# A graph layer that gathers rows by POOL and fetches single rows by SP and ACT: 74 single rows a step instead of 24

## The chip, the core and the metric

One core of a Trainium2 chip runs the whole program. The metric is the time of one execution on the device in microseconds (us), of which the median over several runs is given. One execution is taken with the hardware profiler, and the lines shown come from it. Engines: PE multiplies matrices, DVE and ACT work on vectors, POOL issues the indirect gathers, SP and ACT issue plain transfers; each engine works through its own instructions in their order, and the engines wait for one another by semaphores.

## The reference

There are 50,000 nodes with 128 numbers each and 1,650,000 edges, sorted by their destination; the last of each node's edges is that of the node to itself. Every edge has one of two types, which chooses the weights of its message.

```python
def _L0_gnn_ref(X, edge_index, edge_types, W_data, b_data, W_control, b_control, W_self, b_self):
    src, dst = (edge_index[0], edge_index[1])
    Xs = X[src]
    m_data = Xs @ W_data.T + b_data
    m_ctrl = Xs @ W_control.T + b_control
    msg = jnp.where((edge_types == 0)[:, None], m_data, m_ctrl)
    agg = jax.ops.segment_sum(msg, dst, num_segments=X.shape[0])
    out = agg + (X @ W_self.T + b_self)
    return jax.nn.relu(out)
x = _layernorm(x + _L0_gnn_ref(x, edge_index, edge_type_2, ...), axis=-1)
```

## The kernel before

The edges are cut into blocks, a block into two steps (`Q = 2`). A step sums the rows of its edges' sources by destination and type, and for this it needs these rows of `x` in SBUF. Its edges come by three ways:

- 12 x 128 edges are **gathered**: POOL issues one indirect transfer for 128 rows (L478), 24 of them in a block. A pass is 6 gathers into one tile `y`, of which there are 10, and PE multiplies each 128 rows with a matrix of zeros and ones (`oh`) that says where a row belongs (L497).
- `F = 43` edges are **fillers**. An edge of a node to itself needs no gather, since that row lies in the block's window of `x_t`; DVE puts a filler in its place in the lists (`fill`, L310 to L340).
- `S` edges are **single rows**: SP and ACT fetch each with a transfer of its own, 512 bytes (L452). `TURNS` says how many rows of a step each of the two takes, here 12 and 12.

The single rows' numbers are loaded for ten blocks at a time (`one_g`, L166). DVE makes byte addresses of those of one block (`offsets`, tile `at_x`, L436), a list of `X = Q * S` whole numbers on one partition, at partition `AT`: first SP's for both steps, then ACT's. In `single_rows` each queue loads its addresses from this list into registers (L447, one instruction for a stretch of the list) and then, for each row, sets a register and issues the copy. `LOADS` cuts this work into parts. With `LOADS = 1` each queue does it in one stretch, for a block that is `AHEAD = 2` blocks later. PE waits for both queues' rows of a block at the end of its first step (`rows_fetched`, L461) and multiplies them with one more part of `oh` (L503).

Blocks 0 and the last are plain: they have neither fillers nor single rows. The number of blocks follows from how many edges one holds:

```python
CE = Q * SIZE                      # SIZE = 12 * 128
BE = CE + Q * F + X
NBLK = 2 + (E - CE) // BE
```

The order of every engine's work is written out by hand in the loop over the blocks (L615). In block b, four passes run. After the first, PE does the layer of block b - 1 (`layer`, L528), DVE its moments and the matrix `oh` of block b + 2. After the second come ACT's root of block b - 1 (`root`, L552) and DVE's `counts`. After the third come DVE's `store` of block b - 1 (L558, which reads the root) and its `fill` of block b + 5. After the fourth, DVE makes the addresses for block b + 3 (`offsets`). Part k of the single rows of block b + 2 is issued after pass k. SP also loads the window of `x_t` for block b + 3 (L407, with five base registers every five blocks, L401), the edge lists once in ten blocks (L166 to L175, L302, L307) and stores the rows of block b - 1 (L564).

```python
            if q < LOADS and not plain(b + AHEAD):
                single_rows(b + AHEAD, q)
```

Of the kernel before, what the change touches and what calls it, by code (L numbers as in the profile page):

```python
# [12 lines left out]
F32 = mybir.dt.float32  # L13
# [11 lines left out]
D = 128  # L25
# [9 lines left out]
R = 12  # L35
W = 60
Q = 2
# [1 line left out]
B = 112  # L39
C = R * Q  # L40
F = 43
TURNS = (12, 12)
S = sum(TURNS)
LOADS = 1
AT = 96
X = Q * S
R1 = R + 1
C1 = Q * R1
SIZES = [P] * R
SIZE = sum(SIZES)  # L50
CE = Q * SIZE
BE = CE + Q * F + X
NBLK = 2 + (E - CE) // BE
# [29 lines left out]
def plain(b):  # L83

    return b == 0 or b >= NBLK - 1
# [6 lines left out]
def straight(ctx, tc, c, x, x_t, src_t, dst_t, etype_t, src_f, dst_f, etype_f, src_x, dst_first, first_p, out):  # L92
# [21 lines left out]
    stp = ctx.enter_context(tc.tile_pool(name="stp", bufs=3))  # L114
# [49 lines left out]
    def load_edges(g):  # L164
        t = eds.tile([AT + 1, GB * X], I32, name="one_g")[AT:, :]
        nc.sync.dma_start(t, src_x[None, g * GB * X:(g + 1) * GB * X])  # L166
        one_g[g] = t
        loads[g] = {}
        for name, a in (("s", src_t), ("d", dst_t), ("t", etype_t)):
            t = eds.tile([P, GB, C1], I32, name=name, bufs=1)  # L170
            nc.sync.dma_start(t.rearrange("p b c -> p (b c)"), a[:, g * GC:(g + 1) * GC])
            loads[g][name] = t
        for name, a in (("sf", src_f), ("df", dst_f), ("tf", etype_f)):
            t = eds.tile([GS, F], I32, name=name, bufs=1)
            nc.sync.dma_start(t, a[g * GS:(g + 1) * GS, :])  # L175
            loads[g][name] = t
# [196 lines left out]
    def chunks_of(b, q):  # L373

        n = RCH if b == NBLK - 1 else C if b < NBLK else 0
        return range(q * R, max(q * R, min((q + 1) * R, n)))

    def column(k):
        return k // R * R1 + k % R
# [13 lines left out]
    bys, pcs, zs, pls, bases, ats, ys = {}, {}, {}, {}, {}, {}, {}  # L393
    ohs, cnts, accs, xTs, pos, hs, mvs, sds, os_ = {}, {}, {}, {}, {}, {}, {}, {}, {}
# [22 lines left out]
    def counts(b):  # L417

        cnt = ohp.tile([P, Q, 2 * W], BF16, name="cnt")
        with nc.allow_low_precision(reason="whole numbers up to R1"):  # L420
            nc.vector.tensor_reduce(cnt, ohs[b].rearrange("p (q r) w -> p q w r", r=R1), AX.X, ALU.add)  # L421
        cnts[b] = cnt
# [3 lines left out]
    ROW_SLOTS = AHEAD + 2  # L426
# [4 lines left out]
    def offsets(b):  # L431

        if not plain(b):
            g, i = divmod(b, GB)
            ats[b] = stp.tile([AT + 1, X], I32, name="at_x", bufs=AHEAD + 2)[AT:, :]
            nc.vector.tensor_scalar(ats[b], one_g[g][:, i * X:(i + 1) * X], float(ROW), None, op0=ALU.mult)  # L436

    def single_rows(b, part):

        if part == 0:  # L440
            ys[b] = stp.tile([AT + S, Q, D], F32, name="yx", bufs=ROW_SLOTS)[AT:, :, :]
        both = []
        for j, (eng, dma) in enumerate(((SP, nc.sync), (ACT, nc.scalar))):
            n = Q * TURNS[j]
            k0, k1 = part * n // LOADS, (part + 1) * n // LOADS
            at = Q * sum(TURNS[:j])
            _, rows = nc.values_load_multi_w_load_instructions(ats[b][0:1, at + k0:at + k1], engines=[eng], **RANGE)  # L447
            both.append([(dma, fetched[j][b % ROW_SLOTS], *divmod(k0 + k, TURNS[j]), sum(TURNS[:j]), row)
                         for k, row in enumerate(rows)])
        for pair in zip_longest(*both):  # L450
            for dma, sem, q, k, at, row in filter(None, pair):
                copy = dma.dma_start(ys[b][at + k:at + k + 1, q, :].bitcast(U8), x_bytes[:, bass.ds(row, ROW)])  # L452
                copy.then_inc(sem, 16)
                tc.no_tile_sem_insts.add(copy.ins.name)
                tc.add_to_no_dep_group(f"single{b}", copy.ins)

    def rows_fetched(b):

        times = len(range(b % ROW_SLOTS or ROW_SLOTS, b + 1, ROW_SLOTS))
        for j in range(2):  # L460
            wait = nc.tensor.wait_ge(fetched[j][b % ROW_SLOTS], 16 * Q * TURNS[j] * times)  # L461
        tc.declare_fence(wait.ins, group=f"single{b}")
# [9 lines left out]
    def gathers(b, ks):  # L472
        i = pass_no[0] % SLOTS
        pass_no[0] += 1
        y = gat.tile([P, PASS, D], F32, name="y")
        for k in ks:
            r = REST_ROWS[k] if b == NBLK - 1 else SIZES[k % R]
            copy = nc.gpsimd.indirect_dma_start(  # L478
                out=y[:r, k % PASS, :].bitcast(U8), out_offset=None, in_=x_rows,
                in_offset=bass.IndirectOffsetOnAxis(ap=idxs[b][:r, column(k):column(k) + 1], axis=0))  # L480
            copy.then_inc(landed[i], 16)
            tc.no_tile_sem_insts.add(copy.ins.name)
            tc.add_to_no_dep_group(f"rows{b}_{ks[0]}", copy.ins)
        seen[i] += 16 * len(ks)
        wait = nc.tensor.wait_ge(landed[i], seen[i])  # L485
        tc.declare_fence(wait.ins, group=f"rows{b}_{ks[0]}")
        return y

    def products(b, q, ks):
        y = gathers(b, ks)  # L490
        of_step = chunks_of(b, q)
        if ks[0] == of_step[0]:
            accs[b, q] = ps.tile([P, 3, W], F32, name="acc")
        acc = accs[b, q]
        for k in ks:
            r = REST_ROWS[k] if b == NBLK - 1 else SIZES[k % R]
            nc.tensor.matmul(acc[:, :2, :].rearrange("p t w -> p (t w)"), y[:r, k % PASS, :], ohs[b][:r, column(k), :],  # L497
                             start=k == of_step[0], stop=plain(b) and k == of_step[-1])
        if ks[-1] == of_step[-1]:
            if not plain(b):  # L500
                if q == 0:
                    rows_fetched(b)
                nc.tensor.matmul(acc[:, :2, :].rearrange("p t w -> p (t w)"), ys[b][:, q, :],  # L503
                                 ohs[b][AT:AT + S, q * R1 + R, :], start=False, stop=True)
            for t in range(2):
                nc.tensor.matmul(acc[:, 2, :], to_row[:, t, :], cnts[b][:, q, t * W:(t + 1) * W],  # L506
                                 start=t == 0, stop=t == 1)
# [96 lines left out]
    for b in range(1, RAHEAD):  # L604
        fill(b)
        left_out_columns(b)
        left_out_matrix(b)
        if b < AHEAD:
            onehot(b)
            counts(b)  # L610
            for part in range(LOADS):
                single_rows(b, part)
        if b == 1:
            clear_sums()
    for b in range(NBLK + 1):  # L615
# [16 lines left out]
        for q, (step, ks) in enumerate(passes_of(b)):  # L632
            if ks:
                products(b, step, ks)
# [24 lines left out]
            if q == 3:  # L659
                left_out_matrix(b + RAHEAD)  # L660
                offsets(b + AHEAD + 1)
            if q < LOADS and not plain(b + AHEAD):
                single_rows(b + AHEAD, q)
# [338 lines left out]
```

## Time and profile before

| what | value |
| --- | --- |
| time, median of 3 runs | 15468.53 us (15468.02 to 15471.34) |
| the profiled execution's own time | 15468.53 us |
| its span, first to last instruction | 15466.8 us |
| instructions | 165309 |
| PE busy | 8387.4 us (54%) |
| DVE busy | 11141.1 us (72%) |
| POOL busy | 11673.6 us (75%) |
| ACT busy | 155.0 us (1%) |
| granted TensorE clock, mean | 0.530 |
| DMA engines, mean busy share | between 0.2 and 0.3 in every fortieth of the span |

Register loads, waits and the issue of transfers are not counted as busy, so ACT's 1% and SP's missing row don't tell how long these two queues are occupied; the instructions by line and the timeline do. A line of the groups reads: source line, engine, operation, output tile from input tiles, count | busy us, mean ns of one | idle us of the engine just before them, and what ended most of it. "issue" means that the engine waited for nothing that the profile shows. A "q" behind an engine's name is its sequencer.

### The profile page before, as it was taken

Reading aid. Unit: us, or ns where it says so; the run is one execution under the profiler, and the core shown is the slowest. Engines: PE = TensorE matmul, PEld = TensorE weight load, DVE = VectorE, ACT = ScalarE, POOL = GpSimd, SP = SyncE. Lnnn points to the kernel's source line nnn. Section 1 sums busy time; section 2 is a strip of 40 time slices with the busy share of each in tenths; the row PEclk is TensorE's granted clock in tenths of the full one; section 3 lists DMA queues with packets and bytes.
Section 4 is the critical chain, followed back from the end, with each engine's and each line's share of the span. In section 5 each row is a group of like instructions: output and inputs, shape, how many; then the busy total and the mean of one; then the engine's idle time right before and its main releaser. Section 6 shows DMA issues by size and latency. Waiting matters only on the chain. (4 is left out here: it accounts for less than half of the span.)

```text
span 15466.8 us, 165309 instructions
## 1 busy us (share of the span) xinstructions
PE 8387.4 (54%) x36190; PEld 7171.1 (46%) x36191; DVE 11141.1 (72%) x14143; ACT 155.0 (1%) x521; POOL 11673.6 (75%) x12364
## 2 busy tenths in 40 slices
PE   3555555555555555555555555555555555555555
PEld 3444444444444444444444444444444444444444
DVE  8777777777777777777777777777777777777775
ACT  0000000000000000000000000000000000000000
POOL 7777777777777777777777777777777777777777
PEclk7555555555555555555555555555555555555555
DMA  2222222222222222222222222222222222222222
GB/s 64 61 60 61 60 61 60 61 61 60 61 61 60 61 60 61 60 61 61 60 61 60 61 60 61 61 60 61 60 61 60 61 61 60 61 60 61 60 61 56
DMA packets 622781, 938.16 MB, mean 61 GB/s; under 512 B 314619, under 2 KB 417330, under 8 KB 621772
## 3 DMA queue, kind: packets, MB, share of 16 engines
q0 software_dynamic: 395392, 810.40, 18.5%
q1 hardware_dynamic: 201318, 110.54, 2.7%
q10 hardware_dynamic: 25062, 6.55, 0.2%
q8 instruction: 294, 4.82, 0.1%
q14 instruction: 715, 5.86, 0.1%
HBM read 896.80 MB, written 29.71 MB: 60 GB/s over the span
## 5 line engine op out<-in xcount | busy, mean ns | idle before, releaser
L478 POOL DMA_INDIRECT y<-in_x,idx x12336 | 11654.8, 945 | 3769.4 <-issue 3597.8
L497 PE MATMUL acc<-oh,y 128*128 128x120 f32 x24708 | 5932.4, 430 | 5621.5 <-PEq L485 5621.5
L497 PEld LDWEIGHTS acc<-oh,y 128*128 128x128 f32 x24708 | 5373.0, 327 | 6046.1 <-PEq L485 6032.3
L421 DVE TENSOR_REDUCE cnt<-oh 128x240 bf16<-128x3120 f32 x515 | 2992.3, 5810 | 0.1
L542 DVE COPY h<-po 112x128 f32<-112x128 f32 x515 | 150.2, 292 | 2485.8 <-PE po L536 2471.6
L413 DVE TENSOR_TENSOR oh<-col,small 128x3120 f32<-128x3120 f32 x515 | 1736.3, 3371 | 0.0
L513 DVE TENSOR_TENSOR sums<-acc,sums 128x180 f32 x1030 | 355.9, 346 | 1305.2 <-PE acc L506 1280.1
L339 DVE TENSOR_REDUCE by<-old 128x86 bf16<-128x1118 f32 x513 | 1112.0, 2168 | 17.7
L346 PE MATMUL small<-ones_b,by 128*86 128x1 bf16 x513 | 118.7, 231 | 1335.9 <-DVE by L339 1321.9
L503 PE MATMUL acc<-oh,yx 24*128 24x120 f32 x2052 | 785.6, 483 | 0.0
L346 PEld LDWEIGHTS <-by 128*86 128x86 bf16 x513 | 75.1, 146 | 1414.1 <-DVE by L339 1414.1
L323 DVE TENSOR_TENSOR new<-m,small 128x1118 f32<-128x1118 f32 x513 | 677.3, 1320 | 17.5
L320 DVE TENSOR_TENSOR m<-rk,small 128x1118 f32<-128x1118 f32 x513 | 677.3, 1320 | 17.4
L327 DVE TENSOR_REDUCE v_new<-new 128x26 f32<-128x1118 f32 x513 | 676.1, 1318 | 17.5
L336 DVE TENSOR_TENSOR old<-m,small 128x1118 f32<-128x1118 f32 x513 | 673.4, 1313 | 0.0
L503 PEld LDWEIGHTS acc<-oh,yx 24*128 24x128 f32 x2052 | 502.0, 303 | 213.5 <-issue 209.9
L536 PE MATMUL po<-wmsgT,sums 128*112 128x128 f32 x2060 | 520.5, 396 | 0.0
L536 PEld LDWEIGHTS po<-wmsgT,sums 128*112 128x112 f32 x2060 | 377.8, 253 | 109.5 <-issue 89.5
L534 PE MATMUL po<-bias,sums 3*112 3x128 f32 x1030 | 354.0, 439 | 0.0
L533 PE MATMUL po<-wselfT,xT 128*112 128x128 f32 x1030 | 318.9, 412 | 0.0
L526 DVE TENSOR_TENSOR sums<-pl,sums 128x336 f32<-128x336 f32 x513 | 260.5, 508 | 75.4 <-DVE sums L513 60.6
L552 ACT ACTIVATE sd<-mv,eps 112x1 f32<-112x1 f32 x515 | 151.8, 295 | 15192.2 <-PEq L461 6134.1
(118 smaller groups left out, 4216.2 us busy)
## 6 DMA issues: line engine op xcount, KB each, us to landing
y<-in_x,idx POOLq DMA_INDIRECT x12336
yx<-in_x ACTq DMA_DIRECT2D x12312, 0.5 KB
yx<-in_x SPq DMA_DIRECT2D x12312, 0.5 KB
xT<-in_x_t SPq DMA_DIRECT2D x515, 56.0 KB
out<-o SPq DMA_DIRECT2D x515, 56.0 KB
vf_all<-vd SPq DMA_DIRECT2D x52, 430.0 KB
s<-in_src_t SPq DMA_DIRECT2D x52, 130.0 KB
d<-in_dst_t SPq DMA_DIRECT2D x52, 130.0 KB
```

The lines of the kernel that those rows point to most:

```text
L320: nc.vector.tensor_tensor(m, rk_g[g][:, i, :, None].to_broadcast([P, C1, F]), rank_no_ps[:, None, :].to_broadcast([P, C1, F]), op=ALU.is_e ...
L323: nc.vector.tensor_tensor(new.rearrange("p (q r) f -> p q r f", r=R1), m.rearrange("p (q r) f -> p q r f", r=R1), vf.rearrange("p (q f) -> ...
L327: nc.vector.tensor_reduce(v, new, AX.X, ALU.add)
L336: nc.vector.tensor_tensor(old, m, cb[:, :, None].to_broadcast([P, C1, F]), op=ALU.mult)
L339: nc.vector.tensor_reduce(by, old.rearrange("p (q r) f -> p q f r", r=R1), AX.X, ALU.add)
L413: nc.vector.tensor_tensor(oh, col_g[g][:, i, :, None].to_broadcast([P, C1, 2 * W]), num_ps[:, None, :].to_broadcast([P, C1, 2 * W]), op=AL ...
L421: nc.vector.tensor_reduce(cnt, ohs[b].rearrange("p (q r) w -> p q w r", r=R1), AX.X, ALU.add)
L478: copy = nc.gpsimd.indirect_dma_start(out=y[:r, k % PASS, :].bitcast(U8), out_offset=None, in_=x_rows, in_offset=bass.IndirectOffsetOnAxis ...
L497: nc.tensor.matmul(acc[:, :2, :].rearrange("p t w -> p (t w)"), y[:r, k % PASS, :], ohs[b][:r, column(k), :], start=k == of_step[0], stop= ...
L503: nc.tensor.matmul(acc[:, :2, :].rearrange("p t w -> p (t w)"), ys[b][:, q, :], ohs[b][AT:AT + S, q * R1 + R, :], start=False, stop=True)
L513: nc.vector.tensor_tensor(part, accs.pop((b, q)), part, op=ALU.add)
L536: nc.tensor.matmul(po, a[:, t, :B], c["wmsgT"][:, t * D:(t + 1) * D], start=False, stop=t == 1)
```

## The change

A step has 74 single rows instead of 24, 36 by SP and 38 by ACT. Each queue issues them in three parts, after the first, second and third pass, each part with its own load of addresses. The block's list of addresses has 148 numbers instead of 48 and lies at partition 64 instead of 96. The fetched rows lie at partitions 0 to 73 instead of 96 to 119, and so do their rows of `oh`. The fillers stay 43.

```diff
-TURNS = (12, 12)
+TURNS = (36, 38)
 S = sum(TURNS)
-LOADS = 1
-AT = 96
+LOADS = 3
+AT = 64
 X = Q * S
...
         if part == 0:
-            ys[b] = stp.tile([AT + S, Q, D], F32, name="yx", bufs=ROW_SLOTS)[AT:, :, :]
+            ys[b] = stp.tile([S, Q, D], F32, name="yx", bufs=ROW_SLOTS)
...
                 nc.tensor.matmul(acc[:, :2, :].rearrange("p t w -> p (t w)"), ys[b][:, q, :],
-                                 ohs[b][AT:AT + S, q * R1 + R, :], start=False, stop=True)
+                                 ohs[b][:S, q * R1 + R, :], start=False, stop=True)
...
-        cols[1:NBLK - 1, :, R, AT:AT + S] = steps[:NBLK - 2, :, SIZE + F:]
+        cols[1:NBLK - 1, :, R, :S] = steps[:NBLK - 2, :, SIZE + F:]
```

The parts are cut in `single_rows`, whose text is unchanged:

```python
            n = Q * TURNS[j]
            k0, k1 = part * n // LOADS, (part + 1) * n // LOADS
            at = Q * sum(TURNS[:j])
```

## The prediction

> **What bounds the kernel now.** I read the page's costliest groups first, then the waits of POOL.
>
> ```profile
> L478 POOL DMA_INDIRECT y<-in_x,idx x12336 | 11654.8, 945 | 3769.4 <-issue 3597.8 <-DVE h L543 85.3 <-DVE mv L547 29.5
> ```
>
> ```profile
> POOL y L478 <- issue: 3603.3, 11816, 0.3
> ```
>
> POOL issues one gather after another. Each takes 945 ns, the next follows 0.3 us later, and that pause is "issue": POOL waits for nobody. From the first gather (3.2 us) to the last (15447.8 us) 12,354 gathers (18 read their list from another tile) stand 1.2503 us apart. A block has 24, so it lasts 30.01 us, and 515 blocks fill the span. DVE (72% busy) and PE (54%) have room. Only fewer gathers, or something that becomes slower than 30.01 us a block, can move the time.
>
> SP and ACT issue the single rows. Their busy time is not counted, so I read the issues by line (duration ns min/median/max) and ACT's timeline (start us, us).
>
> ```profile
> L447 ACTq TENSOR_LOAD <-at_x x513: 1647/1668/1785, 16.8 to 15333.3; - x171
> L447 SPq TENSOR_LOAD <-at_x x513: 1579/1585/1679, 26.8 to 15333.7; - x171
> ```
>
> ```profile
> L452 ACTq MOVE yx<-in_x x12312: 29/29/38, 18.6 to 15342.8; - x199
> L452 ACTq DMA_DIRECT2D yx<-in_x x12312: 227/228/536, 18.7 to 15342.8; - x199
> ```
>
> ```profile
> 8029.23 7.77 ACTq L452 DMA_DIRECT2D yx<-in_x  x24
> 8037.10 0.30 ACT L552 ACTIVATE sd<-mv,eps 112x1 f32<-112x1 f32 x1 [29.93 <-PEq L461]
> ...
> 8058.62 8.07 ACTq L452 DMA_DIRECT2D yx<-in_x  x24
> ```
>
> A queue loads 24 row addresses into registers (1.6 us) and then issues 24 row copies. Over all 513 blocks, from the start of the load to the end of the last row, ACT takes 9.83 us and SP 9.66 us; a row after the first costs 0.326 us on ACT, 0.331 on SP (a register move, the copy, and now and then 0.3 us for fetching instructions). So the queues are idle two thirds of the time today.
>
> **The change: fewer gathers.** A step takes 1536 + 43 + 74 edges instead of 1536 + 43 + 24, a block 3306 instead of 3206. With 3072 edges in block 0 that makes 2 + 1646928 // 3306 = 500 blocks instead of 515, and 499 x 24 + 5 = 11,981 gathers. POOL alone would need 11,981 x 1.2503 = 14,980 us, with 3 us ahead and 19 behind 15,002. PE and DVE do the same work per block (a weight load of 74 rows where there were 24, an address conversion of 148 numbers where there were 48: 0.1 us, beside POOL), hidden under POOL. Moving the single rows from partition 96 to 0 costs nothing. The list's partition 64 is only where the addresses are read.
>
> **SP.** It issues 72 rows in three parts of 24: 3 x 9.66 = 28.99 us. Its other issues, from the gaps in its trace, come to 0.61 (store), 0.54 (window), 0.27 (base registers, a fifth of 1.34) and 0.37 (a tenth of 3.7 for the edge lists): 30.78 us a block. That is already more than POOL's 30.01.
>
> **ACT.** It issues 76 rows in parts of 25, 25 and 26. Three parts as today make 29.49; four more rows 4 x 0.326 = 1.30; the root's ACTIVATE between two parts 0.09 (the program's last register load on ACT starts 24 ns after an ACTIVATE); the wait instruction of 0.06 falls away in parts two and three: -0.12. Sum 30.76, before the loads themselves are looked at.
>
> **The loads.** ACT's addresses begin at number 72 of the block's list, so its parts begin at 72, 97 and 122, or at bytes 288, 388 and 488. 288 is a multiple of 16; the other two are not. SP's begin at bytes 0, 96 and 192, and today's two loads at 0 and 96: all multiples. The trace has one load that begins at all places: SP's load of five base registers, which moves on by 20 bytes each time. Four in a row:
>
> ```profile
> L401 SPq TENSOR_LOAD <-base_i x1: 724/724/724, 7117.4 to 7117.4; - x1
> ...
> L401 SPq TENSOR_LOAD <-base_i x1: 1268/1268/1268, 7267.3 to 7267.3; - x1
> ...
> L401 SPq TENSOR_LOAD <-base_i x1: 1288/1288/1288, 7417.8 to 7417.8; - x1
> ...
> L401 SPq TENSOR_LOAD <-base_i x1: 1333/1333/1333, 7567.4 to 7567.4; - x1
> ```
>
> The first begins at a multiple of 16 bytes. Of all 103, the 26 that do take 724 to 809 ns, the 77 others 1244 to 1386, whether they are off by 4, 8 or 12. The loads of one register tell what one costs:
>
> ```profile
> L944 ACTq TENSOR_LOAD <-bad x1: 467/467/467, 15458.9 to 15458.9; - x1
> ...
> L944 SPq TENSOR_LOAD <-bad x1: 471/471/471, 15460.1 to 15460.1; - x1
> ```
>
> ```profile
> L510 DVEq TENSOR_LOAD <-place_i x1030: 298/304/556, 83.6 to 15446.5; - x172
> ```
>
> My reading: from a 16-byte boundary four registers are read at once, otherwise one by one. Aligned, 24 registers are six reads, and (1585 - 471) / 5 = 223 ns for each after the first; unaligned, 5 registers are five reads, (1282 - 471) / 4 = 203 ns. DVE's single loads begin at every multiple of 4 bytes and nearly all take 304 ns, so being off costs nothing by itself: it's the number of reads. ACT's reads are slower in the ratio (1668 - 467) / (1585 - 471) = 1.08. Unaligned, 25 registers take 467 + 24 x (203 to 219) = 5.34 to 5.72 us and 26 take 5.54 to 5.94, where 1.67 was counted. I take the middles: +3.86 and +4.07, with +0.2 for the 25th register of the aligned part: 8.13 us a block.
>
> One surcharge is uncertain: the only ACT load that directly follows a row is the second here.
>
> ```profile
> L447 ACTq TENSOR_LOAD <-at_x x2: 1699/1742/1785, 16.8 to 27.0; - x2
> ```
>
> It took 1785 instead of 1668, and its rows 325 ns instead of 318. For parts two and three that is between 0 and 2 x 0.117 + 49 x 0.007 = 0.58; I take 0.25. ACT's block is then 30.76 + 8.13 + 0.25 = 39.14 us, beyond POOL and SP.
>
> Two rules of the Trainium skill would make the change a gain. "DMA: Bandwidth & Descriptors", section Latency and other measured facts, puts a register load's floor at about 600 ns; with three such loads ACT's block would be an estimated 27.6 us and SP's 27.8, both below POOL, and the time 15,004. The rows above are 0.47 to 1.79 us, and the measurement decides. The same page, section Issuing engines are not separate DMA queues, says that starting a DMA is usually small beside the DMA. Here it is the reverse:
>
> ```profile
> q10 hardware_dynamic: 25062, 6.55, 0.2%
> ```
>
> 0.2% of 16 engines' span over ACT's 25,062 packets is some 20 ns each, and a row's issue is 318.
>
> **Who waits.** The root's ACTIVATE stands behind ACT's first part of rows, two blocks ahead. DVE's store (L558) waits for it, and behind it on DVE lie the list's next addresses. After the root, DVE needs 10 us to those addresses (17 in one block of ten), and ACT asks for them 29 us later, so ACT itself never waits: its issue time is the period. POOL stops when its ten buffers are full.
>
> **The sum.** As today the third block's addresses come at 104.1 us, after 1.3 us for ACT's table rows 3 to 498 follow: 105.4 + 496 x 39.14 = 19,519. Behind the last row come the end of block 498, block 499 and the store: 34 us, from the tail's durations. Span 19,553; the profiled execution took 15,468.5 with a span of 15,466.8, so 2 us more: 19,555. (That execution is the median of the three.)
>
> **Rivals.** *A fixed price for an unaligned load*: about 0.55 us, as 1282 against 740. Then ACT's block is 30.76 + 0.7 (a seventh read in all three) + 1.1 + 0.25 = 32.8, and the time 105.4 + 496 x 32.8 + 36 = 16,410. For it: only loads of five are seen. Against: DVE's single loads pay nothing. 0.07. *ACT's loads don't mind where they begin*: 30.76 + 0.7 + 0.25 = 31.7, or 15,860; only SP and DVE show the effect. 0.05. *Faster, POOL stays the bound*: if a load ran beside the rows before it, ACT's block would be 76 x 0.326 + 1.7 = 26.5, and 15,004 follows; it decides as soon as the slower queue's block falls under 30.9, where 500 blocks take as long as 515 today. Against: ACT's second load began after the last row, and its first row came 1.9 us later. 0.04. Both effects cancelling to within 31 us: 0.01. That the blocks are not fewer is excluded by the count.
>
> **Numbers.** My forecast has 0.83. Its ends: below, reads at 203 ns, no surcharge and none of the rows' jitter (0.15 a block): 38.4, or 19,190, less 140 us for start and tail. Above, 1282 / 5 = 256 ns for every unaligned register: 6.4 and 6.7 us, with the full surcharge 41.3, or some 20,600, cut a little since the dearest reads and the full surcharge need not meet. Range 19,050 to 20,450; the other cases together are under 0.2. A difference of 0.2% (31 us) is about what can be told from none: faster 0.04, same 0.01, slower 0.95.
>
> **What would show it.** ACT's second and third load of a block at 5.3 to 5.9 us, its first at 1.9; rows still 318 ns apart; POOL waiting for PE some 9 us a block; DVE's reciprocal (L558) waiting for ACT; SP's loads near 1.6. Loads under 2.5 us would prove the forecast wrong.

## The result, and the profile after

The changed kernel takes 19,693.3 us, the median of four runs (19,582.6, 19,587.0, 19,799.7 and 19,800.4), against 15,468.3 us before: a ratio of 1.273, with a 95% interval of 1.263 to 1.283. The four runs lie in two pairs 1.1% apart, for which no profile shows a reason; the profile is of the lower pair (time 19,582.6 us, span 19,580.9), and the numbers below are compared with the forecast's 19,555 us through it.

First the page's head and its chain of waits: shares of the span by engine, then by engine and line.

```profile
span 19580.9 us, 261977 instructions
...
ACTq 85%; issue 13%; ACT 1%; DVE 1%; PE 0%; DMA 0%; SPq 0%; DVEq 0%
ACTq L452 52%; ACTq L447 33%; ACT sd L552 1%; DVE cnt L421 0%; PE acc L497 0%; DVE by L339 0%; ACTq L552 0%; DVE new L323 0%; DVE m L320 0%; DVE v_new L327 0%; DVE old L336 0%; DVE oh L413 0%; PE po L536 0%; DMA first_i<-in_dst_first 0%; PE po L534 0%
```

The end is set by ACT's queue and by almost nothing else: its row copies (L452), its register loads (L447), and "issue", the pauses between its own instructions. An engine that the page counts as 1% busy is the bound. The loads' 33% of the chain are some 6,460 us, or 13.0 us for each of 498 blocks with single rows; by their own records they take 13.45 us a block.

The issues by line (ns, min/median/max) show which loads are long. SP's 1,494 loads stay between 1.6 and 1.9 us; ACT's go from 1.9 to 6.0.

```profile
L447 ACTq TENSOR_LOAD <-at_x x1494: 1889/5598/6038, 16.9 to 19540.5; - x187
L447 SPq TENSOR_LOAD <-at_x x1494: 1578/1677/1903, 27.1 to 19509.0; - x187
```

```profile
L452 ACTq DMA_DIRECT2D yx<-in_x x37848: 227/228/693, 19.0 to 19554.9; - x200
```

The row copies themselves are what they were, 228 ns, and a row still follows the one before after 318 ns. Three neighbouring loads of ACT (three windows of the trace), those of 25 registers from byte 388, of 26 from byte 488, and of 25 from byte 288, which is a multiple of 16:

```profile
L447 ACTq TENSOR_LOAD <-at_x x1: 5561/5561/5561, 8038.3 to 8038.3; - x1
...
L447 ACTq TENSOR_LOAD <-at_x x1: 5815/5815/5815, 8052.6 to 8052.6; - x1
...
L447 ACTq TENSOR_LOAD <-at_x x1: 1999/1999/1999, 8067.1 to 8067.1; - x1
```

ACT's timeline (start us, us, idle before in brackets) has one root a block, and the distance of two roots is the period:

```profile
8038.26 0.29 ACT L552 ACTIVATE sd<-mv,eps 112x1 f32<-112x1 f32 x1 [38.72 <-issue]
8043.96 33.39 ACTq L452 DMA_DIRECT2D yx<-in_x  x76
8077.74 0.29 ACT L552 ACTIVATE sd<-mv,eps 112x1 f32<-112x1 f32 x1 [39.18 <-issue]
```

The root now waits for "issue", that is for the rows queued ahead of it on ACT; before, the greater part of its 15192.2 us of idle time was put down to PE's queue. Who waits behind ACT is seen in the groups and in POOL's and DVE's waits (total us, times, longest):

```profile
L478 POOL DMA_INDIRECT y<-in_x,idx x11976 | 11304.8, 944 | 8194.6 <-PE acc L497 4449.5
...
L558 DVE RECIPROCAL rstd<-sd 112x1 f32<-112x1 f32 x500 | 82.0, 164 | 6678.0 <-ACT sd L552 6678.0
```

```profile
POOL y L478 <- PE acc L497: 4449.5, 646, 11.0
POOL y L478 <- issue: 3332.9, 10915, 0.3
```

```profile
DVE rstd L558 <- ACT sd L552: 6678.0, 498, 25.2
```

A gather still takes 944 ns, and its "issue" pause is still 0.3 us. New is that POOL waits for buffers that PE hasn't freed: 8194.6 - 3332.9 = 4861.7 us, or 9.8 us a block. DVE waits 13.4 us a block for ACT's root, and the next lists of addresses, PE and POOL follow behind it.

### The profile page after: what moved, and what is told of

Read it like the earlier page. It is cut to its first block, busy times and chain, and to the rows that moved or that the text cites. A ratio compares the mean times of both kernels' runs of the same rounds, so it can differ in the third digit from the quotient of the medians.

```text
span 19580.9 us, 261977 instructions
## 1 busy us (share of the span) xinstructions
PE 5715.8 (29%) x35101; PEld 5373.9 (27%) x35102; DVE 10810.8 (55%) x13719; ACT 150.5 (1%) x506; POOL 11310.9 (58%) x11991
## 4 chain that ended last, share of the span: by engine, by line
ACTq 85%; issue 13%; ACT 1%; DVE 1%; PE 0%; DMA 0%; SPq 0%; DVEq 0%
ACTq L452 52%; ACTq L447 33%; ACT sd L552 1%; DVE cnt L421 0%; PE acc L497 0%; DVE by L339 0%; ACTq L552 0%; DVE new L323 0%; DVE m L320 0%; DVE v_new L327 0%; DVE old L336 0%; DVE oh L413 0%; PE po L536 0%; DMA first_i<-in_dst_first 0%; PE po L534 0%
## 5 line engine op out<-in xcount | busy, mean ns | idle before, releaser
L478 POOL DMA_INDIRECT y<-in_x,idx x11976 | 11304.8, 944 | 8194.6 <-PE acc L497 4449.5
L497 PE MATMUL acc<-oh,y 128*128 128x120 f32 x23962 | 4166.1, 345 | 0.1
L497 PEld LDWEIGHTS acc<-oh,y 128*128 128x128 f32 x23962 | 3925.1, 255 | 0.3
L558 DVE RECIPROCAL rstd<-sd 112x1 f32<-112x1 f32 x500 | 82.0, 164 | 6678.0 <-ACT sd L552 6678.0
L421 DVE TENSOR_REDUCE cnt<-oh 128x240 bf16<-128x3120 f32 x500 | 2896.5, 5793 | 0.1
L413 DVE TENSOR_TENSOR oh<-col,small 128x3120 f32<-128x3120 f32 x500 | 1685.7, 3371 | 0.0
L503 PE MATMUL acc<-oh,yx 74*128 74x120 f32 x1992 | 457.2, 318 | 0.0
L503 PEld LDWEIGHTS acc<-oh,yx 74*128 74x128 f32 x1992 | 380.6, 237 | 0.0
L269 PEld LDWEIGHTS <-ones_b 128*128 128x128 bf16 x600 | 75.6, 149 | 1091.3 <-issue 1080.2
```

Of the source, the lines that this page charges most:

```text
L413: nc.vector.tensor_tensor(oh, col_g[g][:, i, :, None].to_broadcast([P, C1, 2 * W]), num_ps[:, None, :].to_broadcast([P, C1, 2 * W]), op=AL ...
L478: copy = nc.gpsimd.indirect_dma_start(out=y[:r, k % PASS, :].bitcast(U8), out_offset=None, in_=x_rows, in_offset=bass.IndirectOffsetOnAxis ...
```

## The experiments

Two theories of the load stood against each other. **Reads**: from a 16-byte boundary four registers are read at a time, otherwise one by one, on any queue. **Fixed price**: a load that doesn't begin at such a boundary costs some 0.55 us more, however long it is. A third is left from the rivals: that something else than the place makes ACT's loads long (ACT itself, or the crowd of rows).

One thing has to be known before the times are read. All experiments ran on later occasions, on four chips (which chip the first results came from isn't on record), and there the kernel *before* itself took 18,039, 18,208, 18,062 and 18,054 us where it had taken 15,468. Ratios are therefore to the kernel before on the same chip. What differs there is dealt with after the fourth experiment.

**1. The same list four bytes later, in the kernel before.** Nothing else is changed: 24 registers a load, one load a block and queue; the list grows to 52 numbers to make room. (Line numbers are 3 higher.)

```diff
+XL = 52
+CUTS = ((0, 24), (0, 24))
+STARTS = ((1,), (25,))
...
-            k0, k1 = part * n // LOADS, (part + 1) * n // LOADS
-            at = Q * sum(TURNS[:j])
-            _, rows = nc.values_load_multi_w_load_instructions(ats[b][0:1, at + k0:at + k1], engines=[eng], **RANGE)
+            k0, k1 = CUTS[j][part], CUTS[j][part + 1]
+            at = STARTS[j][part]
+            _, rows = nc.values_load_multi_w_load_instructions(ats[b][0:1, at:at + k1 - k0], engines=[eng], **RANGE)
```

> The kernel before with one change: the list of 48 addresses begins 4 bytes later, so that both queues' only load of 24 registers begins beside a multiple of 16 bytes. Theory, one by one: SP's load goes from 1.59 to about 5.1 us, ACT's from 1.67 to about 5.4; both queues have 20 us a block to spare, so the time stays within 0.2% of 15,468. Rival, the loads of the changed kernel are long because of the crowd: 1.6 and 1.7 us here. Rival, a fixed price: 2.1 and 2.2 us.

Measured: 18,160.8 against 18,038.9 us, ratio 1.0071 (1.0057 to 1.0085). Its register loads, issues by line:

```profile
L450 ACTq TENSOR_LOAD <-at_x x513: 5252/5287/5362, 16.9 to 18095.8; - x171
L450 SPq TENSOR_LOAD <-at_x x513: 2434/5039/5132, 27.8 to 18102.9; - x171
```

The same 24 registers took 1,668 and 1,585 ns from bytes 0 and 96 (the kernel before) and take 5,287 and 5,039 from bytes 4 and 100. That is (5287 - 467) / 23 = 210 ns for each register after the first on ACT and (5039 - 471) / 23 = 199 ns on SP. The fixed price, which gives 2.1 to 2.2 us, falls. So does the idea that ACT alone shows it, or the crowd of rows: SP does too, with 24 rows a block. The time was expected within 0.2% and came 0.7% higher. In this run DVE waits for ACT's root in a third of the blocks (waits of DVE: total us, times, longest), which in the first profile of the kernel before it did once, for 0.4 us:

```profile
DVE rstd L561 <- ACT sd L555: 1354.4, 173, 17.1
```

How long the unshifted kernel waits there on this occasion wasn't profiled, so where the 0.7% comes from isn't shown.

**2. The long queue swapped.** SP gets 38 rows and ACT 36, so that ACT's parts begin at bytes 304, 400 and 496 (all multiples of 16) and SP's at 0, 100 and 200.

```diff
-TURNS = (36, 38)
+TURNS = (38, 36)
```

> The changed kernel with 38 rows a step by SP and 36 by ACT. All of ACT's parts of 24 now begin at multiples of 16 bytes (304, 400, 496), and SP's parts of 25, 25 and 26 begin at 0, 100 and 200. Theory, one by one: ACT's loads 1.7 to 1.8 us, SP's 1.9, 5.45 and 5.65; SP becomes the bound with a block of about 40.0 us, the time about 20,000 us, and PE waits for the rows instead of DVE for the root. Rival, the price belongs to ACT or to its place in the order: the time falls to about 15,600 us with SP's loads under 2 us.

Measured: 27,783.6 us, ratio 1.540 (1.537 to 1.543). The time isn't what was expected; the loads and the chain are:

```profile
L447 ACTq TENSOR_LOAD <-at_x x1494: 3/1664/2014, 17.6 to 27669.0; - x187
L447 SPq TENSOR_LOAD <-at_x x1494: 1089/5206/5723, 29.2 to 27745.1; - x187
```

```profile
SPq 67%; issue 29%; DMA 2%; PE 1%; DVE 1%; another core or an unknown queue 0%; PEldq 0%; DVEq 0%; ACT 0%; ACTq 0%
```

The long loads went to the other queue, and that queue became the bound. SP's three parts have medians of 1.83, 5.22 and 5.53 us, ACT's of 1.66, 0.69 and 1.77 (the records of the middle part are cut short by what is told after experiment 4). It is the place in the list, not the queue.

**3. The changed kernel with every part begun at a multiple of 16 bytes**, by gaps in the list. The rows, blocks and parts stay.

```diff
+XL = 156
+CUTS = ((0, 24, 48, 72), (0, 25, 50, 76))
+STARTS = ((0, 24, 48), (72, 100, 128))
...
-            k0, k1 = part * n // LOADS, (part + 1) * n // LOADS
-            at = Q * sum(TURNS[:j])
+            k0, k1 = CUTS[j][part], CUTS[j][part + 1]
+            at = STARTS[j][part]
```

> The changed kernel with its rows, parts and loads as they are (ACT's parts of 25, 25 and 26 rows); only the list of addresses gets filler numbers so that every load begins at a multiple of 16 bytes. Theory, registers are read one by one when a load does not begin at such a place: ACT's second load falls from 5.60 to about 2.0 us and its third from 5.85 to about 2.25, ACT's block from 39.2 to 32.0 us, the time to about 16,015 us. Rival, three loads in a row or the crowd of rows is what makes the loads long: they stay near 5.7 us and the time stays at 19,600 to 19,800. Rival, a fixed price of about 0.55 us for a load that begins elsewhere: the loads fall by 0.55 us each and the time by some 550 us.

Measured: 25,449.9 us, ratio 1.412 (1.409 to 1.414), where 16,015 us was expected. The loads did as they should:

```profile
L450 ACTq TENSOR_LOAD <-at_x x1494: 3/1930/2462, 17.6 to 25306.2; - x187
L450 SPq TENSOR_LOAD <-at_x x1494: 3/1607/1875, 29.2 to 25365.5; - x187
```

ACT's 5.6 and 5.85 us are gone, and ACT is no longer the bound (SP's queue has 58% of the chain). But the time is longer than that of the changed kernel on the first occasion, which can't come from shorter loads.

**4. Fewer rows, every part aligned**: 32 rows by SP and 34 by ACT, parts cut at multiples of four.

```diff
-TURNS = (36, 38)
+TURNS = (32, 34)
...
-            k0, k1 = part * n // LOADS, (part + 1) * n // LOADS
+            k0, k1 = (p * n // LOADS // 4 * 4 for p in (part, part + 1))
```

> 32 single rows a step by SP and 34 by ACT, parts cut at multiples of 4 rows, so that all loads begin at multiples of 16 bytes; 502 blocks and 12,040 gathers. Theory: SP's block comes to about 27.9 us and ACT's to 28.2, both under POOL's 30.01, so POOL is the bound again: about 15,080 us, 2.5% faster than the kernel before. Rival, rows issued all through the block slow POOL or PE as well: POOL's gathers stand further apart than 1.250 us, and the time stays above 15,300 us.

Measured: 23,404.9 us, ratio 1.297 (1.294 to 1.300); none of its loads is long (medians 1,687 and 877 ns). Missed by far again.

**What was different.** The shortest records of those runs gave it away: loads of 3 ns, row copies of 1 ns. SP's and ACT's records stand still for about 0.7 us at a time, often on both queues at once, and what began in that time is recorded with a few ns. In the shifted list's run, 6,286 copies and register moves of SP and 4,128 of ACT last 0.6 to 1.5 us; in the first profile of the kernel before, 2 and 0. Of ACT's 4,128, 2,307 end within 50 ns of one of SP's. So 24 rows of a block, 7.77 us in ACT's timeline of the kernel before, become (experiment 1, timeline of ACT):

```profile
8031.00 17.56 ACTq L455 DMA_DIRECT2D yx<-in_x  x24
```

Whether that belongs to one chip is seen when the padded list and the 32/34 version run on a second one, here with a version that removes the misalignment by taking two rows a step from ACT (parts of 24 everywhere):

```diff
-TURNS = (36, 38)
+TURNS = (36, 36)
```

> The padded list again (every load of the changed kernel begins at a multiple of 16 bytes, all else as it is), since the first time the kernel before took 18,039 us where it takes 15,468 elsewhere, and there both queues' instructions stood still in steps of about 0.7 us. Where the kernel before takes 15,468 us: by the theory ACT's loads 2.0, 2.0 and 2.25 us, ACT's block 32.0 us, the time about 16,015 us. If the queues' standing still belongs to issuing rows all through the block, and not to that chip, the time is above 19,000 us again.

> 32 and 34 single rows a step, all loads at multiples of 16 bytes, again on another occasion. By the theory SP's block is 27.9 us and ACT's 28.2, POOL's 30.01 is the bound, the time about 15,080 us where the kernel before takes 15,468. If rows issued all through the block make the queues stand still on every chip, above 18,000 us.

> 36 single rows a step by SP and 36 by ACT, three parts each. No other edit: 2 of 38 rows fewer for ACT, and by that ACT's parts begin at 288, 384 and 480 bytes, all multiples of 16; 500 blocks. Theory: ACT's loads 1.7 to 1.8 us instead of 2.0, 5.6 and 5.85, its block about 29.8 us; SP's block is 28.9 for rows and 1.9 for the rest, 30.8 to 31.0 us, so SP becomes the bound, just above POOL: 104 + 496 x 30.9 + 30 = 15,460 us, within 1% of the kernel before. Rival, the loads are long because ACT issues many rows: two rows fewer a step save 4 x 0.33 us a block, and the time is about 19,000 us.

Measured, beside 18,207.8 us for the kernel before: padded 25,791.5 us, ratio 1.416 (1.414 to 1.419); 32/34 23,715.1, 1.302 (1.299 to 1.304); 36/36 25,343.1, 1.393 (1.391 to 1.395). The second of these chips behaves like the first of them. The loads of 36/36 answer to the theory of reads: 24 registers from bytes 288, 384 and 480, all short.

```profile
L447 ACTq TENSOR_LOAD <-at_x x1494: 3/1672/1975, 17.1 to 25180.6; - x187
L447 SPq TENSOR_LOAD <-at_x x1494: 3/1608/1899, 33.4 to 25250.5; - x187
```

**5. The changed kernel itself, beside its padded version.** On a third chip the unedited changed kernel ran with the padded list and 32/34.

> The changed kernel itself, beside the padded list and the 32 and 34 rows on one chip. Where the kernel before takes 15,468 us: 19,580 to 19,800 us. Where it takes 18,000 to 18,200 and the queues stand still in steps of 0.7 us: by the theory the standing still is paid for each row and record, so this kernel takes about as long as the padded one there, 25,400 to 25,800 us; the 7.3 us of long loads a block are then time in which the other queue catches up. If the loads cost the same there as well, it is some 3,600 us slower than the padded one.

> The padded list, as before: 16,015 us by the theory where the kernel before takes 15,468; 25,400 to 25,800 where it takes 18,000 to 18,200. In both cases ACT's loads are 2.0, 2.0 and 2.25 us or less.

> 32 and 34 rows a step, all loads at multiples of 16 bytes: 15,080 us by the theory where the kernel before takes 15,468; 23,300 to 23,800 where it takes 18,000 to 18,200.

Measured, beside 18,062.0 us: changed 25,798.4 us, ratio 1.429 (1.426 to 1.432); padded 25,480.7, 1.411 (1.408 to 1.414); 32/34 23,437.2, 1.298 (1.296 to 1.301). This settles the puzzle of experiment 3: not the padding was slow, the occasion was, for the changed kernel grew from 19,693 to 25,798 us as well. Its register loads didn't; the first two lines are of the changed kernel there, the third of the padded one:

```profile
L447 ACTq TENSOR_LOAD <-at_x x1494: 863/5524/6075, 17.6 to 25753.3; - x187
L452 ACTq DMA_DIRECT2D yx<-in_x x37848: 1/228/1413, 19.7 to 25767.8; - x200
```

```profile
L450 ACTq TENSOR_LOAD <-at_x x1494: 3/1922/2507, 17.7 to 25343.1; - x187
```

The rows grew. Within a part, ACT's rows stand 0.335 us apart on the mean in the first profile, whether SP issues a row within 1 us of them or not; here it is 0.534 us when SP does and 0.331 when it doesn't. ACT's second part, which runs mostly alone, takes 14.0 and 14.2 us on the two occasions; the first and third take 16.4 and 21.0 us, where they took 10.5 and 14.6. The chains, first of the changed kernel there, then of the padded one:

```profile
ACTq 72%; issue 25%; DVE 1%; ACT 1%; PE 0%; another core or an unknown queue 0%; DMA 0%; SPq 0%; DVEq 0%
```

```profile
SPq 60%; issue 36%; DMA 2%; DVE 1%; PE 1%; ACTq 0%; PEldq 0%; another core or an unknown queue 0%; ACT 0%; DVEq 0%
```

So in these surroundings shorter loads on ACT only hand the bound to SP's queue, and aligning is worth 1.2% (25,798 to 25,481). The 19% that the first profile's sums say for it (below) can't be seen here.

**6. The loads by themselves**, three times over, unpadded and padded. The row copies are left out, and one copy a block and queue brings other rows in their place.

```diff
+            for _ in range(REPEAT):
+                nc.values_load_multi_w_load_instructions(ats[b][0:1, at + k0:at + k1], engines=[eng], **RANGE)
```

> The changed kernel with its loads alone: each part's load of addresses is done three times, and the row copies are left out; one copy a block and queue brings other rows of x in their place, so the messages of the single rows are left out. So few instructions remain on SP and ACT that they should not stand still on any chip. Theory: ACT's nine loads a block are 3 x (1.9 + 5.5 + 5.75) = 39.5 us, with gaps, the copy and the root 40.5 us, ACT is the bound and the time 105 + 496 x 40.5 + 36 = about 20,230 us. Rival, a load hides behind others, or is short without rows around it: under 30 us a block, POOL is the bound, about 15,000 us.

> The same with the padded list, so that all nine loads begin at multiples of 16 bytes: 3 x (1.9 + 1.9 + 2.15) = 17.9 us a block on ACT, POOL's 30.01 is the bound, about 15,000 us. The messages of the single rows are left out here too. If the price hangs on anything but where a load begins, this one takes as long as the other.

Measured, beside 18,054.0 us: 17,171.9 us, ratio 0.951 (0.950 to 0.953), and 17,178.3, 0.952 (0.950 to 0.953). As a trial of the loads it failed: nothing used the registers, and the program that ran has semaphore events where the loads should be.

```profile
L448 ACTq EVENT_SEMAPHORE  x4482: 13/17/22, 17.0 to 17094.8; - x195
L448 SPq EVENT_SEMAPHORE  x4482: 1/17/2098, 31.0 to 17080.4; - x195
```

It tells something else. With hardly an instruction on SP and ACT, POOL's sum of 15,002 us should have been the time; the span was 17,152.9, SP still had 622 copies and register moves of 0.6 to 1.5 us, and POOL waited for something outside of what the profile names ("remote"; waits of POOL: total us, times, longest):

```profile
POOL y L478 <- remote: 1182.4, 404, 4.6
```

So the standing still of the later occasions also comes without single rows, though the versions with many rows lose most. Whether it is the chips, the occasion or something else stays open.

## Why the prediction was right

The mechanism and the size held. By its own steps, measured in the first profile after as means over 498 blocks:

| step | predicted | measured |
| --- | --- | --- |
| ACT's load for the third block | 104.1 us | 104.5 us |
| ACT's loads of a block | 1.87 + 5.53 + 5.74 us | 2.00 + 5.60 + 5.85 us |
| surcharge after a row | 0.25 us | in the loads; none on the rows |
| ACT's block (the period) | 39.14 us | 39.22 us |
| SP's three parts | 28.99 us | 28.92 us |
| POOL waiting for buffers, a block | about 9 us | 9.8 us |
| behind the last row | 34 us | 25.7 us |
| span | 19,553 us | 19,580.9 us |

**POOL.** Gathers of 944 ns and 0.3 us apart, 500 blocks: the fewer gathers came as counted, and POOL had the time to spare. They bought nothing because POOL stopped being the bound.

**The loads.** This was the step that all hung on, and it was read from a load of five registers and loads of one, none of 25. Per register after the first it measured (5.60 - 0.467) / 24 = 0.214 us, inside the 0.203 to 0.219 that the text gave. Experiment 1 confirms the rule at 24 registers on both queues, experiment 2 that it moves with the place. The measured loads are 0.3 us longer together than predicted; the surcharge covers nearly that, because a load that directly follows a row is longer: SP's take 1.585 us in the first part, behind a wait, and 1.69 in the two others. The other part of the surcharge, 325 ns instead of 318 a row, didn't exist: the median distance stayed 318, and 325 was only a matter of the first rows of the program. That the period came within 0.2% is therefore partly luck: a part that was too small (the loads') and one that wasn't there (the rows') nearly made up for each other.

**The sum.** About +38 us for the period (496 blocks), -8 for the tail (the one term that was clearly too big) and -1 for the start are the 28 us between the forecast span and the measured one. The median of the four runs is 0.6% above the profiled execution.

**The rivals.** The fixed price (16,410 us) fell in experiment 1, in which 5,287 ns stand against 2,200. "ACT's loads don't mind" (15,860) fell with the first profile. A load beside the rows (15,004) was contradicted by the timeline: 76 rows with two loads among them in 33.4 us and 5.7 us to the next row, one after the other; none of ACT's 1,494 loads begins before the row ahead of it has ended. The register load's floor of about 600 ns in the Trainium skill, "DMA: Bandwidth & Descriptors", section Latency and other measured facts, taken as the price of a load, would have made a gain of the change. In the profile after, no load of 24 to 26 registers took under 1.578 us, and the long ones took nine to ten times the floor; the loads of one register that the prediction shows are below it, at 0.47 us on SP and ACT and 0.30 on DVE.

One comparison of the prediction is of unlike things: 20 ns is a packet, and ACT's 12,312 rows make about two packets each (25,062). A row's DMA work is then some 40 ns, still an eighth of the 318 of its issue.

What isn't shown: that alignment alone gives the time back on the first occasion. By the first profile's own rows, ACT's block would fall from 39.22 us by the loads' 13.45 less the 6.1 of the padded version's (1.99, 1.90 and 2.23 us in one block), and the span by 496 x 7.33 = some 3,640 us to an estimated 15,940 us, still above the kernel before since ACT's rows remain. No version that was run and has all messages beats the kernel before; the estimate for 32/34, 15,080 us, couldn't be tried in the surroundings that it is for.

## What to carry to other kernels

Begin each slice of a register load at a multiple of four whole numbers, and when a list is cut into parts by a division, write down at which byte each part begins: two rows a step more on one queue made two of its three loads some 4 us longer here (5.60 and 5.85 us, where 24 registers from a multiple of 16 bytes take 1.67 to 1.77). Count what a queue issues (here 0.32 us a row, and 0.2 us for each read of a register load, of one register or of four) as work of that queue, though the profile calls it idle; with work moved off a busy engine, the queue that takes it is the next bound. And run the unedited kernels beside an experiment: only that told a changed occasion from an edit that costs.

## What was not expected of the hardware

The same kernel took 15,468 us on the first occasion and 18,039 to 18,208 us on four chips later, and the changed one 19,693 and 25,798, at a granted clock for PE that is only a little lower for the changed kernel (0.605 and 0.581). SP and ACT stand still there, often together, some 0.7 us at a time, and the cause is open; a register load read one by one is as long as before (5,524 ns against 5,598, medians of all ACT's loads). The price of a misaligned load goes by the number of its registers: 24 took 5.3 us on ACT, where the same 24 from a multiple of 16 bytes took 1.67 (six reads of four, by the theory of reads).
